# Layer 2 of a four-layer megakernel: who adds the exponentials, and in what order the small work beside them stands

## Chip, core and metric

The kernel runs on one core of one Trainium2 chip, as one launch. The metric is device time in microseconds, as the median of several executions. The tuned kernel before the change takes 3455.24 us (three runs, 3453.64 to 3456.24).

## What is computed

Input and output are `x` of shape (4, 256, 48, 48) in float32: four samples, 256 channels, 2304 positions. Four layers follow one another, each of the form x = x + layer(groupnorm(x)), with 32 groups and no affine part:

```python
# layer 0: attention with 8 heads of 64, q and k normalized, scale 10
sim = einsum('bhdi,bhdj->bhij', q, k) * 10; out = einsum('bhij,bhdj->bhid', softmax(sim), v)
# layer 1: 3x3 max pool, blur with stride 3 to 16x16, four depthwise 11x3 filters,
#          sigmoid gate, gate enlarged to 48x48 and multiplied onto the input
# layer 2: attention with one head of 64 (theta, phi, g), then W and batch norm over all samples
f = einsum('bnc,bcm->bnm', theta_x, phi_x) * 64 ** -0.5; y = einsum('bnm,bmc->bnc', softmax(f), g_x)
# layer 3: channel gate from means, depthwise 3x3, instance norm, leaky relu
```

The softmax is computed without subtracting a maximum: exponentials are multiplied with the values, and the result is divided by the sum of the exponentials.

## The kernel before

The attention of layers 0 and 2 is one long loop, `attend` (line 487). A unit is one block of 384 queries: in layer 0 for a pair of heads (96 units), in layer 2 for two query halves of one sample (12 units, three for each sample). A unit has nine groups of two key blocks of 128 keys. The pass for a group `t` issues, in this order: the scores of group `t` (`scores`, line 318: eight matmuls a key block pair on TensorE, one exponential of 128x768 for each block on ScalarE into one of eight `pt` buffers), then `add_up` of the group before (line 349: the sum of exponentials over the keys, kept elementwise in `acc`), then the jobs that are due, then the fills, and last `weigh` of the group before (line 337: exponentials times values). All engines run in this written order; nothing is reordered later. The fills are everything else: projections of the next pair or sample, layer 1 of other samples, group norms, statistics. A job in `due` or `fills` carries a rank; without one it is 5, and jobs of a pass are sorted by it. Only fills of a rank below 1 stand ahead of `add_up`; `lanes` are generators that are advanced by a step or more in each pass.

`add_up` has two forms. For a group in `paired`, GpSimd adds the group's two exponential tiles into `half` (line 355) and VectorE adds `half` to `acc` (line 370). For the others VectorE adds both tiles itself. In layer 0, sample 0 pairs the odd groups and samples 1 to 3 pair none. In layer 2, samples 0 to 2 pair all nine groups and sample 3 the odd ones (`l2_unit`, line 1293). The first addition of a unit is line 364.

At the end of a unit, `last` (line 462) copies the weighed values from PSUM (`take`), and places the rest: `total` (line 374) sums `acc` over partitions with matmuls and `invert`, `fold` and `divide` follow on VectorE and GpSimd with DMAs between. The last sample's units are "soon": `total_here` (line 425) sums `acc` with a matrix of ones and takes a reciprocal on VectorE. The very last unit is also "final"; its `total_here` folds and copies the row of sums on ScalarE ahead of the reciprocal.

Layer 1 of samples 0 to 2 runs beside layer 0. That of sample 3 runs beside layer 2 of samples 0 to 2, in four lanes (`l1_last`, line 1371): maxima and blur on VectorE (`maxima`, line 878), the filters as matmuls (`strips_pe`, line 999) on shifted copies that DMAs on SP's queue place in one of three buffers ("y", "t" and "w" in `ORDER3`, line 992), then `gated` (line 1123) and statistics for the next group norm. After that `follow` (line 1427) starts the layer 2 projection of sample 3 (`project2`, line 1151: `both` makes theta and phi from one product, `g` the values). The projection of sample 0 runs beside the last pair of layer 0, one slice of 384 positions in every ninth pass; there the slices come by DMA from a DRAM copy (`fetch`).

`w_stats` (line 1262) multiplies finished `y` with W into both `pj` PSUM tiles (there are only two) and takes VectorE's batch statistics of them. After the loop, the last unit's product, the merge of statistics and layer 3 follow.

Of the attention's inputs, `biased` (line 577) puts its one-column product into a column of the key projection's tile when `of_k` says that this tile belongs to the current pass, and into a tile of its own otherwise.

Of the kernel before, what the change touches and what calls it, by code (L numbers as in the profile page):

```python
# [78 lines left out]
def usual_path(  # L79
# [269 lines left out]
    def add_up(u, g):  # L349

        pts = [u["pt"][j] for j in range(g * G, (g + 1) * G)]
        terms = u.setdefault("terms", [])
        if g in u["paired"]:
            half = hpool.tile([P, 2, SL], F32, tag="half", name="half")
            nc.gpsimd.tensor_add(half, pts[0], pts[1])  # L355
            pts = [half]
            ready, u["terms"] = terms, pts
        else:
            ready, u["terms"] = terms + pts, []
        if g == NG - 1:  # L360
            ready, u["terms"] = ready + u["terms"], []
        if "acc" not in u and len(ready) > 1:
            u["acc"] = apool.tile([P, 2, SL], F32, tag="acc", name="acc")
            nc.vector.tensor_add(u["acc"], ready[0], ready[1])  # L364
            ready = ready[2:]
        if "acc" not in u:
            u["terms"] = ready + u["terms"]
            return
        for term in ready:
            nc.vector.tensor_add(u["acc"], u["acc"], term)  # L370
# [54 lines left out]
    def total_here(u):  # L425

        ps = pj_tile()
        for h, c in enumerate(HALVES):
            nc.tensor.matmul(ps[c, :SL], lhsT=ones, rhs=u["acc"][:, h, :], start=True, stop=True)
        u["rinv"] = rpool.tile([P, SL], F32, tag="rinv", name="rinv")  # L430
        if u.get("final"):
            fold(u, nc.vector)
            row = xsp.tile([P, NK, SL + 1], F32, tag="xs", name="lrow")[:, 0, :SL]
            nc.scalar.copy(row, ps[:, :SL])
        nc.vector.reciprocal(u["rinv"], ps[:, :SL])
        u["l"] = row if u.get("final") else ps

    def note(u):

# [22 lines left out]
    def last(u, t):  # L462

        take(u)
        if u.get("soon"):
            todo = [
                (fills, 1, lambda: total_here(u)), (due, 2, lambda: divide(u, nc.vector)),
            ]
            if u.get("final"):
                noted.append(lambda: note(u))  # L470
            else:
                todo.insert(1, (due, 2, lambda: fold(u, nc.vector)))
                todo.append((due, 2, lambda: note(u)))
            after = 3
        else:
            at_total = AT_TOTAL if "shift" in u["of"] else AT_CHUNK
            todo = [
                (fills, at_total, (4.1, lambda: total(u))), (due, AT_FOLD, lambda: fold(u, nc.gpsimd)),
                (due, AT_INVERT, lambda: invert(u)),
                (due, AT_DIVIDE, lambda: divide(u, nc.gpsimd)),  # L480
            ]
            after = AT_AFTER
        todo += [(fills, after, fn) for fn in u["after"]]
        for when, dt, fn in todo:
            when.setdefault(t + dt, []).append(fn)

    def attend(phases):


        groups = []  # L490
        for units, work, others in phases:
            for slot, fns in work.items():
                fills.setdefault(len(groups) + slot, []).extend(fns)
            st = {"others": [[gen, n, a, z, 0, 0] for gen, n, a, z in others], "at": 0}
            groups += [(u, g, st) for u in units for g in range(NG)]
        prev = None

        def lanes(some, st, t, ends):
            for lane in some:
                gen, n, a, z, done, ready = lane  # L500
                until = -(-n * (st["at"] + 1 - a) // (z - a))
                clock["final"] = final = st["at"] == z - 1
                while final or (done < until and t >= ready and not ends):
                    wait = next(gen, None)
                    if wait is None:
                        break
                    done, ready = done + 1, t + wait
                lane[4:] = done, ready

        def do(table, t, which=lambda rank: True):  # L510

            jobs = [job if isinstance(job, tuple) else (5, job) for job in table.pop(t, ())]
            table[t] = [job for job in jobs if not which(job[0])]
            for rank, fn in sorted((job for job in jobs if which(job[0])), key=lambda job: job[0]):
                fn()

                if rank in EVICTED:
                    take_taps(1)

        for t, (u, g, st) in enumerate(groups):  # L520
            for j in range(g * G, (g + 1) * G):
                scores(u, j)

            do(fills, t, lambda rank: rank < 1)
            if prev is not None:
                add_up(*prev)
            do(due, t)

            ends = prev is not None and prev[1] == NG - 1
            clock["t"], clock["slot"] = t, st["at"] % NG  # L530

            clock["early"] = True
            if clock["slot"] == AT_AFTER % NG:
                lanes([lane for lane in st["others"] if lane[1] == FREE], st, t, ends)
            do(fills, t)
            clock["early"] = False
            lanes(st["others"], st, t + 0.5, ends)
            st["at"] += 1
            if prev is not None:
                pu, pg = prev  # L540
                for j in range(pg * G, (pg + 1) * G):
                    weigh(pu, j)
                if pg == NG - 1:
                    last(pu, t)
            take_taps(QUOTA[clock["slot"]])
            prev = (u, g)
        pu, pg = prev
        add_up(pu, pg)
        for j in range(pg * G, (pg + 1) * G):
            weigh(pu, j)  # L550
        last(pu, len(groups))
        for t in sorted(set(due) | set(fills)):
            do(fills, t)
            do(due, t)
# [385 lines left out]
    def strips(b, k, norm, res):  # L940
# [50 lines left out]
    ROUNDS3 = (((0, 6), (6, 9)), ((9, 15),), ((15, 18),), ((18, 21),))  # L991
    ORDER3 = [
        (0, 1, "y"), (0, 2, "y"), (0, 3, "y"), (0, 0, "t"), (1, 1, "w"), (1, 0, "t"), (1, 2, "w"),
        (1, 3, "t"),
    ]
    FILLS_AT_ONCE = 8
    SETTLED = 3
# [122 lines left out]
        add()  # L1120
        yield 1

    def gated(b, k, norm, res):

        acc = res["acc"]
        gate = lp.tile([P, AS, AS], F32, tag="gate", name="gate")
        nc.vector.tensor_scalar(
            acc, acc, vec[:, V_M1, k : k + 1], inv1[:, k : k + 1], ALU.subtract, ALU.mult
        )
        yield 1  # L1130
        nc.scalar.activation(gate, acc, AF.Exp, bias=nb1[:, k : k + 1], scale=-1.0)
        yield 1
        nc.vector.tensor_scalar(gate, gate, 1.0, None, ALU.add)
# [9 lines left out]
        for i in range(4):  # L1143
            if i < 3:
                nc.vector.tensor_mul(xg[:, :, i], xg[:, :, i], up)
            if i > 0:
                nc.vector.tensor_add(xg[:, :, i - 1], xg[:, :, i - 1], up2)
            yield 1


    def project2(b, norm, s2):
# [43 lines left out]
        def both(s):  # L1195
# [15 lines left out]
                bias=at["bias"][theta, 0:1],  # L1211
            )
            nc.sync.dma_start(s2["k"][theta, cols], s2["k"][phi, cols])

        def g(s):
            ps = pj_tile()
            nj = SL // P
            for i in range(nj):
                for k in range(NK):
                    for c in HALVES:  # L1220
                        nc.tensor.matmul(
                            ps[c, i * D : (i + 1) * D],
                            lhsT=at["x"](s, k)[:, i * P + c.start : i * P + c.stop],
                            rhs=at["w"][:, k, 2, :], start=k == 0, stop=k == NK - 1,
                        )
            nc.scalar.copy(
                s2["v"][:, s * nj : (s + 1) * nj, :].rearrange("p j d -> p (j d)"),
                ps[:, : nj * D],
            )
            if b == 0 and s + 2 < NSL:  # L1230
                fetch(s + 2)

        return start, [
            [(1, lambda s=s: both(s)), (2 if b else 2.7, lambda s=s: g(s))] for s in range(NSL)
        ]

    Y = {}
# [55 lines left out]
    def l2_unit(b, c, s2):  # L1293
        return {
            "pt": {}, "qc": slice(c * SL, (c + 1) * SL), "of": s2, "after": [],
            "paired": PAIRED if b == B - 1 else range(NG), "scale": D ** -0.5,
            "soon": b == B - 1, "final": b == B - 1 and c == L2C - 1,
            "o": lambda: y_of(b)[:, c * SL : (c + 1) * SL],
        }
# [71 lines left out]
    def l1_last(b, ahead):  # L1371
# [29 lines left out]
        def gates():  # L1401
            for k in range(NK):
                yield from until(res[k], "summed")
                yield from gated(b, k, norm, res[k])
                yield from stats(k)
            yield from gn(b, norm2, [], [])

# [19 lines left out]
    def follow(start, slices, norm):  # L1427

        while "nb" not in norm:
            yield 1  # L1430
        yield 2
        start()
        yield 1
        for c in range(L2C):
# [71 lines left out]
    for b in range(B):  # L1506
        work, others = {}, []

        def stats(b, c):
            return [lambda k=k: w_stats(b, k, c) for k in range(NK)]  # L1510

        if b > 0:
            spread(work, stats(b - 1, 1), [4, 5])
# [38 lines left out]
        fn()  # L1552
    for s in range(NCH):
        projs[0]["values"](s)
    projs[1]["norms"]()
    attend(phases)
    last_y = [w_mul(B - 1, k, L2C - 1, wide=True) for k in range(NK)]
# [1477 lines left out]
```

## Time and profile before

| what | value |
|---|---|
| median of three runs | 3455.24 us |
| profiled execution, its own time | 3453.34 us |
| its span, first to last instruction | 3451.5 us |
| TensorE clock granted, mean | 0.997 |
| TensorE busy | 3384.6 us, 98% |
| VectorE busy | 2539.3 us, 74% |
| ScalarE busy | 2297.4 us, 67% |
| GpSimd busy | 828.0 us, 24% |
| exponentials, 128x768, line 330 | 1944 at 810 ns |
| additions of a tile, line 370 | 1368 at 1000 ns |
| additions of a half, line 370 | 171 at 1097 ns |
| pairs on GpSimd, line 355 | 189 at 1966 ns |

In the profile PE is TensorE, DVE VectorE, ACT ScalarE and POOL GpSimd. A group's row gives its line, engine and operation, its output and inputs, the shapes, the number of instructions, their busy time and mean in ns, and then the idle time of the engine ahead of them with what ended it. Busy time of VectorE or GpSimd includes time in which an instruction has begun and is held up. A row of the order of time gives start, duration, engine, line, operation, and in brackets the idle time ahead of it and who ended it. The span ends at 3451.5 us; layer 2's attention runs from 2870.57 to about 3285 us, and layer 3 after it.

### The profile page before, as it was taken

The numbers are of one execution on the slowest core, as the hardware profiler recorded it, in microseconds if no ns is written. First come the engines' busy times: TensorE is split into PE (matmuls) and PEld (weight loads), VectorE is DVE, ScalarE is ACT, GpSimd is POOL, SyncE is SP. The second block draws the span as 40 slices with busy tenths as digits, with TensorE's granted clock in tenths as the row PEclk, the third lists the DMA queues.
The fourth block names the chain that finished last, engine by engine and source line by source line (L and its number), as shares of the span: only waits on it lengthen the run. The fifth ranks groups of instructions, "written<-read, shape, count | busy, mean of one in ns | idle before, by whom it ended". The sixth has DMA issues, their size and how long they took to land. (4 is left out here: it accounts for less than half of the span.)

```text
span 3451.5 us, 89291 instructions
## 1 busy us (share of the span) xinstructions
PE 3384.6 (98%) x37966; PEld 1698.6 (49%) x37966; DVE 2539.3 (74%) x3298; ACT 2297.4 (67%) x3690; POOL 828.0 (24%) x734
## 2 busy tenths in 40 slices
PE   8999999999999999999999999999999999899988
PEld 5555555555545444544454445554444444444533
DVE  3455545568788788687888787878887878857777
ACT  5565655555886687557866885569768855454577
POOL 2433333320111111011110010101010114777434
PEclk9999999999999999999999999999999999999999
DMA  2211111111111111131111011111111110230067
GB/s 91 50 23 27 22 27 22 27 22 27 20 32 22 27 22 22 31 73 22 27 21 24 15 31 18 31 18 27 22 27 18 29 21 8 58 66 11 9 154 229
DMA packets 111593, 127.25 MB, mean 37 GB/s; under 512 B 42912, under 2 KB 101648, under 8 KB 110416
## 3 DMA queue, kind: packets, MB, share of 16 engines
q1 hardware_dynamic: 109936, 119.53, 17.3%
q8 instruction: 300, 4.92, 0.6%
q10 hardware_dynamic: 1248, 1.91, 0.2%
q14 instruction: 109, 0.89, 0.1%
HBM read 56.99 MB, written 11.80 MB: 20 GB/s over the span
## 5 line engine op out<-in xcount | busy, mean ns | idle before, releaser
L330 ACT ACTIVATE pt<-sc 128x768 f32<-128x768 f32 x1944 | 1473.6, 810 | 757.9 <-PE sc L324 751.4
L370 DVE TENSOR_TENSOR acc<-acc,pt 128x768 f32<-128x768 f32 x1368 | 1367.3, 1000 | 145.3 <-ACT pt L330 51.7
L344 PE MATMUL av<-pt,v 64*64 64x384 f32 x13824 | 1274.8, 484 | 0.0
L324 PE MATMUL sc<-q,k 64*64 64x384 f32 x13824 | 1270.0, 482 | 0.5 <-ACT pt L330 0.5
L324 PEld LDWEIGHTS sc<-q,k 64*64 64x64 f32 x13824 | 525.3, 133 | 589.6 <-issue 556.5
L344 PEld LDWEIGHTS av<-pt,v 64*64 64x64 f32 x13824 | 518.2, 133 | 568.4 <-issue 521.5
L421 POOL TENSOR_TENSOR o<-o,rinv 128x384 f32<-128x384 f32 x95 | 123.7, 1302 | 1710.1 <-DMA rinv<-rinv 1700.0
L355 POOL TENSOR_TENSOR half<-pt 128x768 f32<-128x768 f32 x189 | 370.7, 1966 | 488.0 <-ACT pt L330 405.3
L739 DVE SCALAR_TENSOR_TENSOR x<-pj,bo,x 128x384 f32<-128x384 f32 x192 | 118.5, 617 | 344.2 <-ACT row L388 186.9
L951 ACT ACTIVATE prod<-pd,wt 128x256 f32<-128x256 f32 x486 | 340.5, 761 | 0.2
L370 DVE TENSOR_TENSOR acc<-acc,half 128x768 f32<-128x768 f32 x171 | 187.5, 1097 | 167.8 <-POOL half L355 166.7
L625 PE MATMUL pj<-xs,w 128*128 128x384 f32 (+1 forms) x720 | 275.4, 505 | 0.0
L625 PEld LDWEIGHTS pj<-xs,w 128*128 128x128 f32 x720 | 124.1, 189 | 127.9 <-ACT v L664 34.3
L324 PE MATMUL sc<-qv,kd 64*64 64x384 f32 x1728 | 167.3, 492 | 2.9 <-ACT pt L330 2.8
L974 DVE TENSOR_REDUCE prod<-prod 128x256 f32<-128x1280 f32 x114 | 168.7, 1480 | 0.9 <-ACT prod L951 0.9
L344 PE MATMUL av<-pt,qv 64*64 64x384 f32 x1728 | 167.1, 490 | 0.0
L723 PE MATMUL pj<-o,wo 128*128 128x384 f32 (+1 forms) x384 | 161.4, 502 | 2.3 <-DVE x L739 2.0
L659 PEld LDWEIGHTS pj<-w,xs 128*128 128x128 f32 x1080 | 134.4, 191 | 24.2 <-issue 1.2
L364 DVE TENSOR_TENSOR acc<-pt 128x768 f32<-128x768 f32 x99 | 116.4, 1176 | 39.5 <-ACT pt L330 39.4
L659 PE MATMUL pj<-w,xs 128*128 128x128 f32 x1080 | 134.9, 275 | 0.0
L417 POOL TENSOR_TENSOR o<-raw 128x384 f32<-128x384 f32 x95 | 121.6, 1280 | 43.6 <-ACT raw L413 42.5
L413 ACT COPY raw<-av 128x768 f32<-128x768 f32 x108 | 86.4, 800 | 48.2 <-PE av L344 47.7
(304 smaller groups left out, 2227.6 us busy)
## 6 DMA issues: line engine op xcount, KB each, us to landing
xs<-in_x_dram SPq DMA_DIRECT2D x90, 384.0 KB
sh<-pad SPq DMA_DIRECT2D x126, 162.2 KB
rinv<-rinv SPq DMA_DIRECT2D x208, 94.5 KB
out_dram<-x SPq DMA_DIRECT2D x23, 384.0 KB
w<-in_wqkv_dram SPq DMA_DIRECT2D x32, 192.0 KB
x<-in_x_dram SPq DMA_DIRECT2D x4, 1152.0 KB
x<-in_x_dram SPq DMA_DIRECT2D x9, 384.0 KB
rinv<-ls SPq DMA_DIRECT2D x208, 1.5 KB
```

The source lines that it names most:

```text
L324: nc.tensor.matmul(ps[c * D : (c + 1) * D, h, :SL], lhsT=u["of"]["k"][r, j0 : j0 + D], rhs=u["of"]["q"][r, u["qc"]], start=True, stop=True,)
L330: nc.scalar.activation(pt, ps[:, :, :SL], AF.Exp, scale=u["scale"])
L344: nc.tensor.matmul(u["av"][h * D : (h + 1) * D, half, :SL], lhsT=value(u, j, h)[r], rhs=pt[r, h, :], start=j == 0, stop=j == JB - 1,)
L355: nc.gpsimd.tensor_add(half, pts[0], pts[1])
L370: nc.vector.tensor_add(u["acc"], u["acc"], term)
L417: eng.tensor_add(u["sum"], u["raw"][:, 0, :], u["raw"][:, 1, :])
L421: eng.tensor_mul(o, o, u["rinv"])
L625: nc.tensor.matmul(ps[:, :n], lhsT=at["w"][:, k, t, :], rhs=xs[s][:, k, :n], start=k == 0, stop=k == NK - 1,)
L659: nc.tensor.matmul(ps[:, i * P : (i + 1) * P], lhsT=xs[s][:, k, i * P : (i + 1) * P], rhs=at["w"][:, k, 2, :], start=k == 0, stop=k == NK - 1,
L723: nc.tensor.matmul(ps[:, :n], lhsT=wo[:, p, k * P : (k + 1) * P], rhs=o["o"][:, :n], start=True, stop=True,)
L951: nc.scalar.activation(bufs[n % 3][:, :, min(n, 1) + i].rearrange("p (r c) -> p r c", c=AS), pd[:, PAD + dr : PAD + dr + AS, PAD + dc : PA ...
L974: nc.vector.tensor_reduce(to, bufs[n % 3][:, :, : min(n, 1) + len(taps)], AX.X, ALU.add)
```

## The change

There are seven edits.

1. `l2_unit`: no group of layer 2 is paired any more. Every exponential tile is added by VectorE.
2. The last unit: its last group's two tiles are not added at all. `add_up` leaves them in `loose`, and `total_here` sums `acc` and both tiles with the matrix of ones, in six matmuls in one accumulation, issued after the weighing of group 7 and ahead of that of group 8. The copy of the row of sums and the fold come after the take.
3. `ORDER3`: the last shifted stack of sample 3's second half is placed in the "y" buffer instead of the "t" buffers.
4. `gated(brief=True)` for sample 3: four steps are merged into others, so the same instructions are issued over fewer passes; `follow` waits one pass instead of two.
5. `project2` for sample 0: in each slice `g` comes first (rank 1) and `both` second (rank 2.7); the fetch of the slice after next is issued by `both`.
6. `w_stats` of layer 2 gets rank 0.5, so its products and statistics stand ahead of `add_up`.
7. `of_k` is cleared before the second pair's `norms` ahead of the loop.

```diff
@@ add_up
         if g == NG - 1:
             ready, u["terms"] = ready + u["terms"], []
+            if u.get("final"):
+                u["loose"] = ready
+                return
@@ total_here
-        for h, c in enumerate(HALVES):
-            nc.tensor.matmul(ps[c, :SL], lhsT=ones, rhs=u["acc"][:, h, :], start=True, stop=True)
+        terms = [u["acc"], *u.get("loose", ())]
+        for i, term in enumerate(terms):
+            for h, c in enumerate(HALVES):
+                nc.tensor.matmul(
+                    ps[c, :SL], lhsT=ones, rhs=term[:, h, :], start=i == 0,
+                    stop=i == len(terms) - 1,
+                )
         u["rinv"] = rpool.tile([P, SL], F32, tag="rinv", name="rinv")
-        if u.get("final"):
-            fold(u, nc.vector)
-            row = xsp.tile([P, NK, SL + 1], F32, tag="xs", name="lrow")[:, 0, :SL]
-            nc.scalar.copy(row, ps[:, :SL])
         nc.vector.reciprocal(u["rinv"], ps[:, :SL])
-        u["l"] = row if u.get("final") else ps
+        u["l"] = ps
@@ last
         take(u)
+        if u.get("final"):
+            row = xsp.tile([P, NK, SL + 1], F32, tag="xs", name="lrow")[:, 0, :SL]
+            nc.scalar.copy(row, u["l"][:, :SL])
+            u["l"] = row
@@ attend, after the last pass
         add_up(pu, pg)
+        total_here(pu)
@@ ORDER3
-        (1, 3, "t"),
+        (1, 3, "y"),
@@ gated
-        yield 1
+        if not brief:
+            yield 1
...
-            yield 1
+            if not brief or i % 2:
+                yield 1
@@ project2
-            [(1, lambda s=s: both(s)), (2 if b else 2.7, lambda s=s: g(s))] for s in range(NSL)
+            [(1, lambda s=s: both(s)), (2, lambda s=s: g(s))] if b else
+            [(1, lambda s=s: g(s)), (2.7, lambda s=s: both(s))] for s in range(NSL)
@@ l2_unit
-            "paired": PAIRED if b == B - 1 else range(NG), "scale": D ** -0.5,
+            "paired": (), "scale": D ** -0.5,
@@ follow
-        yield 2
+        yield 1
@@ stats
-            return [lambda k=k: w_stats(b, k, c) for k in range(NK)]
+            return [(0.5, lambda k=k: w_stats(b, k, c)) for k in range(NK)]
@@ before the loop
+    of_k.clear()
     projs[1]["norms"]()
```

More of the change, by code (lines that the diff above doesn't have):

```diff
@@ L464, in last @@
         take(u)
+        if u.get("final"):
+            row = xsp.tile([P, NK, SL + 1], F32, tag="xs", name="lrow")[:, 0, :SL]
+            nc.scalar.copy(row, u["l"][:, :SL])
+            u["l"] = row
         if u.get("soon"):
             todo = [
-                (fills, 1, lambda: total_here(u)), (due, 2, lambda: divide(u, nc.vector)),
+                (due, 2, lambda: fold(u, nc.vector)), (due, 2, lambda: divide(u, nc.vector)),
             ]
@@ L471, in last @@
             else:
-                todo.insert(1, (due, 2, lambda: fold(u, nc.vector)))
+                todo.insert(0, (fills, 1, lambda: total_here(u)))
                 todo.append((due, 2, lambda: note(u)))
@@ L1121, in strips_pe, with gated @@
         yield 1
-    def gated(b, k, norm, res):
+    def gated(b, k, norm, res, brief=False):
         acc = res["acc"]
@@ L1213, in both @@
             nc.sync.dma_start(s2["k"][theta, cols], s2["k"][phi, cols])
+            if b == 0 and s + 2 < NSL:
+                fetch(s + 2)
         def g(s):
@@ L1229, in g @@
             )
-            if b == 0 and s + 2 < NSL:
-                fetch(s + 2)
         return start, [
-            [(1, lambda s=s: both(s)), (2 if b else 2.7, lambda s=s: g(s))] for s in range(NSL)
+            [(1, lambda s=s: both(s)), (2, lambda s=s: g(s))] if b else
+            [(1, lambda s=s: g(s)), (2.7, lambda s=s: both(s))] for s in range(NSL)
         ]
@@ L1403, in gates @@
                 yield from until(res[k], "summed")
-                yield from gated(b, k, norm, res[k])
+                yield from gated(b, k, norm, res[k], brief=True)
                 yield from stats(k)
```

## The prediction, on record before the run

> **What bounds the kernel now.** I read the page first, then the stretches of layer 2, then the groups and the order of time inside them. TensorE sets the span:
>
> ```profile
> PE 3384.6 (98%) x37966; PEld 1698.6 (49%) x37966; DVE 2539.3 (74%) x3298; ACT 2297.4 (67%) x3690; POOL 828.0 (24%) x734
> ```
>
> An edit that removes no matmul can therefore give back only TensorE's waits, 67 us at most in the whole span, and slow clock. Where they are, the stretches show (columns: stretch, length, then busy time of PE, PEld, DVE, ACT, POOL, then the granted clock and the DMA share):
>
> ```profile
> 2873.00:3005.00 132.00, 119.43 (x1427) 59.92 (x1421) 120.82 (x134) 64.93 (x98) 95.24 (x48) 0.99 0.16 31
> 3005.00:3202.00 197.00, 184.82 (x2282) 95.96 (x2278) 119.27 (x142) 98.32 (x153) 132.21 (x73) 0.97 0.22 42
> 3202.00:3284.00 82.00, 79.88 (x969) 44.24 (x964) 65.45 (x79) 43.10 (x58) 42.87 (x40) 1.00 0.04 5
> 3284.00:3300.00 16.00, 10.50 (x96) 6.28 (x90) 12.85 (x32) 8.57 (x6) 1.67 (x4) 1.00 0.00 0
> 2460.00:2592.00 132.00, 131.71 (x1440) 65.94 (x1432) 113.29 (x151) 78.86 (x127) 15.14 (x14) 1.00 0.13 20
> ```
>
> The first two are layer 2 of samples 0 to 2, with the last sample's layer 1 beside it; TensorE idles 12.6 and 12.2 us there. The last row is layer 0 with the same kind of layer 1 work, where no pair is added on POOL: 0.3 us of idleness. The difference stands in the groups (first row of each engine: layer 2's first stretch; last row: layer 0, 2400 to 2800 us):
>
> ```profile
> L370 DVE TENSOR_TENSOR acc<-acc,half 128x768 f32<-128x768 f32 x24 | 29.3, 1220 | 3.3 <-POOL half L355 3.0
> L355 POOL TENSOR_TENSOR half<-pt 128x768 f32<-128x768 f32 x33 | 73.5, 2239 | 21.2 <-ACT pt L330 13.0 <-DVE acc L370 8.0
> L370 DVE TENSOR_TENSOR acc<-acc,pt 128x768 f32<-128x768 f32 x217 | 215.6, 994 | 19.0 <-ACT pt L330 4.5 <-DVE acc L370 0.9
> ```
>
> One shape costs 1220 ns beside POOL's pairs and 994 without. In order of time it is plainer:
>
> ```profile
> 3134.54 2.56 DVE L1147 TENSOR_TENSOR x<-x,l1acc 128x768 f32<-128x768 f32 x1
> 3137.03 2.55 DVE L370 TENSOR_TENSOR acc<-acc,half 128x768 f32<-128x768 f32 x1
> 3139.50 1.02 DVE L1264 BATCH_NORM_STATS2 bst<-pj 128x6 f32<-128x384 f32 x2
> 3140.11 2.01 PE L1256 MATMUL pj<-y,Ww 64*64 64x384 f32 x8 [3.51 <-DVE bst L1264]
> ```
>
> Two operations of 0.95 us elsewhere take 2.55 us each, the statistics queue behind them, and TensorE waits 3.51 us for the two pj banks, then runs its next chunks slowly. Comparing TensorE's chunk starts with the usual distance of each kind (1.29 us for 16 attention matmuls), the lost time above 0.25 us sums to 34.7 us from 2873 to 3202: about 16 before 3005 and 18.7 after, slow clock included.
>
> **The Trainium skill.** "SBUF — State Buffer", section "Who interferes with whom", says that a VectorE instruction with two SBUF inputs and a GpSimd instruction that reads SBUF exclude each other, the second being held for the whole first. The 2.55 us against 0.95 agree. "GPSIMD Engine Reference", section 4.1, puts a two-input elementwise operation on GpSimd at about twice VectorE's time; the trace has about 1.8 us for an undisturbed pair against 0.95 to 1.0. "TensorE: Matmul & The Clock Gate", "What's actually happening", says that the clock falls after an idle window; the stretch with the longest waits has 0.97.
>
> **The change, part by part.**
>
> *Pairs.* For samples 0 to 2, nine POOL pairs and nine VectorE additions of a unit become 17 VectorE additions. One add costs 1.0 us (the 994 row). I cost a ledger per group of two key blocks: TensorE's time from the chunk distances, VectorE's from undisturbed rows. For the first 32 groups (2874 to about 3001, 127 us now): TensorE's chunks 112 us. VectorE: 61 adds x 1.0, and 49 us for the rest at undisturbed price (four half maxima of about 8.5 us, statistics, the first reciprocal of 2.5, small items): 110. What POOL still holds comes on top. In the 132 us stretch VectorE was busy 120.8; undisturbed its 28 adds would be 28 and the rest 49, so 44 us were waits, 0.46 us for each of POOL's 95 us. POOL keeps 95.2 - 73.5 = 21.7 us (fold, divide, shift, diagonals), some 9 us of VectorE. So VectorE needs 119 and becomes the limit here, with 2 us in which it waits itself: 121 against 127, **6 us** saved. Bounds: nothing left of the holds and lag absorbed by the eight pt buffers, 11; holds at 0.7 per us, 1.
>
> The second stretch is loaded only at the two gates. There the ledger's lag (adds 2.0 plus the gate's 2.5 us, then three 0.87 us operations a group, against 2.6 to 3.2 us of TensorE) climbs to about 6.4 and 7.5 us. Eight pt buffers let VectorE lag about three groups, 7.7 us, so I charge 2 us there. At the next statistics (lag 5) the two pj banks bind: about 3.5 us for them and the group norm's matmul just after. Unchanged projection waits take 1.3, the last projection 1.3, other small waits 2. That is 10 of 18.7: **8.7 us** saved, bounds 4 and 14.
>
> *Statistics ahead of additions* is what lets me charge so little: two bn_stats (0.94 us) no longer stand behind two adds (2.0). Queued behind them are now the adds; they wait for a product of the same group, with at least two groups of pt buffers to spare. In the last sample the statistics' waits (1.05 and 1.07 us in the trace) and smaller ones shrink, while four added adds per unit lie in VectorE's 16 us of idle time: **1.5 us**, bounds 0 and 3.
>
> *Shorter chain.* The last stack goes to the y buffer, which is free, so its product comes four groups earlier; its 16 DMAs, 11 us of issue on SP's queue, move ahead of two copies of sample 2's keys (kd). Those land about 11 us later, near 3098, and are first read some 8 us after that; without this cover TensorE would wait for them. The gates stand in fewer groups. The group norm's matmul comes eight groups earlier, and the six projections (2.8 us a pair) are spread over three groups instead of standing in one block at 3183. No work goes away; its gain is in the figures above (some 1 us of alternating waits), and its price is the gate lag, charged at 2.
>
> *g first beside layer 0.* TensorE's waits between 2700 and 2870 us:
>
> ```profile
> PE pj L1221 <- ACT qv L1209: 3.7, 6, 0.6
> ```
>
> Six waits of 0.62: ScalarE's two exponentials end about 1.5 us after the scores, two evictions of 0.58 follow, TensorE arrives after 2.08. With g first, TensorE does g (0.85) and an output product (0.74), 1.59 us; g's one eviction of 0.32 ends at about 1.85. The wait becomes 0.26: 6 x 0.36 = **2.2 us**, bounds 0 and 3.7. The fetch moves behind the projection, half a microsecond later in its group; the next slice is used two slots of some 28 us later, so it costs nothing.
>
> *The last total*, in order of time:
>
> ```profile
> 3282.98 0.95 DVE L370 TENSOR_TENSOR acc<-acc,half 128x768 f32<-128x768 f32 x1
> 3284.04 2.02 DVE L370 TENSOR_TENSOR acc<-acc,pt 128x768 f32<-128x768 f32 x2
> 3286.12 0.87 PE L429 MATMUL pj<-acc,ones 128*64 128x384 f32 x4 [1.59 <-DVE acc L370]
> 3287.54 2.56 DVE L435 RECIPROCAL rinv<-pj 128x384 f32<-128x384 f32 x1 [1.01 <-ACT lrow L434]
> ```
>
> Three adds (3 us) leave the chain; TensorE sums two more terms instead (2 x 0.7) ahead of the last weighing. Last exponential 3282.87, totals to 3285.0, reciprocal to 3287.7, weighing and take beside it, then fold, multiply, shift to 3289.2; the 13 warming matmuls (3.2 us) end at 3289.5. The next product starts there instead of at 3291.2: **1.7 us**, bounds 0.5 and 3.
>
> *Clearing of_k* takes another bank for one 1-column product before the attention: 0.
>
> Sum: 6 + 8.7 + 1.5 + 2.2 + 1.7 = 20.1 us. The profiled execution took 3453.34 us (span 3451.5); it becomes 3433.2. The median of the runs is 1.9 us above it: 3435.
>
> **The rivals.**
>
> 1. *All the cover holds.* Removing the holds takes every such wait: of 34.7 us only the projections' and the notes' (about 6) stay, 29 saved, with 1.5, 2.2 and an upper 3: 36, so 3419. For it: layer 0's row, 0.3 us idle with VectorE 113 of 132 busy. Against: the maxima are packed denser here, 119 in 121.
> 2. *The waits move into VectorE's queue.* In the first stretch nothing is saved, the gates' lag costs all but 2 of the second's, and the ends give half: about 4 us, 3451. For it: VectorE was busy 120.8 of 132 already. Against: a third of that was waiting.
> 3. *Slower: VectorE becomes the bound.* If an add stays at the 1.39 us that the paired first adds average in the first stretch, 60 x 0.39 = 23 us come on VectorE's path there, 17 us longer than now; the second loses 5, the ends give 5: 3472. It decides from about 1.33 us an add, where 60 x 0.33 - 6 equals the other gains of 14. Against: adds without an overlapping POOL operation took 1.0 in layer 0.
>
> **How the numbers follow.** Forecast 0.53 (its own range 3425 to 3446), rival 1 0.20, rival 2 0.18, rival 3 0.09. Half of rival 1 below and about as much above are left out: 3417 to 3450. Within 0.2% (6.9 us, about what a measurement of this kernel can tell from no change) lies most of rival 2; faster takes the forecast, rival 1 and the better third of rival 2: 0.80; same 0.13; slower 0.07.
>
> **What would show it.** Adds of layer 2 near 1.0 us; no pairs on POOL; VectorE still above 95% up to the second sample's statistics and TensorE idle about 7 us there; the wait before the last statistics of sample 2 near 3 us; g's waits replaced by about 0.26 us; the last reciprocal about 2.5 us after the last exponential. Wrong if the adds stay above 1.2, or if waits for pt exceed 5 us.

## The result and the profile after

The changed kernel takes 3426.32 us (median of four runs, 3424.51 to 3428.06), beside 3454.44 us for the kernel before on the same chip: ratio 0.9918, 95% interval [0.9901, 0.9936], or 28.1 us less. The forecast was 3435 us, with a range of 3417 to 3450. The profiled execution took 3426.86 us, with a span of 3425.0.

First the engine totals of the profile after:

```profile
PE 3379.8 (99%) x37974; PEld 1684.4 (49%) x37974; DVE 2542.0 (74%) x3389; ACT 2296.0 (67%) x3690; POOL 628.5 (18%) x641
```

TensorE has eight matmuls more and 26 us of span less; GpSimd has lost 93 instructions and 200 us; VectorE has 91 instructions more and is busy only 2.7 us longer. That last pair is the change in small: the added work cost VectorE hardly more than the holding up that it ended. The stretches of layer 2 in the changed kernel, which begins 8 us earlier (columns: stretch, length, busy time of PE, PEld, DVE, ACT, POOL, then clock, DMA share, GB/s):

```profile
2865.00:2992.00 127.00, 122.67 (x1462) 59.96 (x1458) 110.22 (x167) 65.44 (x100) 22.69 (x16) 0.97 0.16 33
2992.00:3178.00 186.00, 178.79 (x2251) 87.20 (x2244) 132.50 (x190) 98.13 (x152) 31.02 (x24) 1.00 0.23 44
3178.00:3257.00 79.00, 77.97 (x958) 35.99 (x952) 65.09 (x90) 43.08 (x58) 19.09 (x28) 1.00 0.04 5
```

TensorE now idles 4.3, 7.2 and 1.0 us there, where it idled 12.6, 12.2 and 2.1. Not all of the gain is idle time: of the 20.0 us that layer 2 gives in the table below, 17.0 are idle time of TensorE (29.6 us before, 12.6 after) and 3.0 are busy time of nearly the same matmuls (4732 and 4741 in the two records). The granted clock is 0.97 in the first stretch, with 4.3 us of idle time of which 3.1 are one wait, and 1.00 in the second, with 7.2 us in waits of at most 1.5; here it went with the longest single wait and not with their sum. VectorE is busy 110.2 of the first 127 us, 87%: it did not become the limit. Its additions over the three stretches together:

```profile
L373 DVE TENSOR_TENSOR acc<-acc,pt 128x768 f32<-128x768 f32 x190 | 187.9, 989 | 35.2 <-ACT pt L330 24.2
```

989 ns an addition, against 1220 ns for a half beside GpSimd's pairs in the first stretch before. TensorE's waits from 2690 to 3275 us (line, releaser: us in total, times, longest):

```profile
PE pj L247 <- DVE lsum L447: 3.1, 1, 3.1
PE pj L1234 <- ACT qv L1220: 2.2, 6, 0.4
PE sc L324 <- ACT pt L330: 1.9, 5, 0.7
...
PE pj L233 <- DVE bst L1276: 1.5, 1, 1.5
...
PE pj L1210 <- ACT qv L1220: 1.3, 3, 0.4
```

The waits for VectorE's batch statistics of layer 2's products (bst), 13.7 us before in three rows, are 1.5; two rows for `acc` that are left out have 1.1 and 1.0. To see where the time went I took four events from the order of time of each kernel: the first attention scores, the first scores of layer 2, the product after the last unit (line 1256 before, 1268 after), and the end of the span. Each cell is the length of a stage in us, in one profiled execution:

| kernel | start to scores | layers 0 and 1 | layer 2 | the rest | span |
|---|---|---|---|---|---|
| before | 44.0 | 2826.6 | 420.6 | 160.3 | 3451.5 |
| changed | 40.0 | 2822.8 | 400.6 | 161.7 | 3425.0 |
| difference | -4.0 | -3.8 | -20.0 | +1.4 | -26.5 |

The medians differ by 28.1, the profiled executions by 26.5; the experiments below show that the last stage alone varies by more than that gap.

### The profile page after: what moved, and what is told of

It reads as the page before. It is cut to its first block, busy times and chain, and to the rows that moved or that the text cites. A ratio compares the mean times of both kernels' runs of the same rounds, so it can differ in the third digit from the quotient of the medians.

```text
span 3425.0 us, 89305 instructions
## 1 busy us (share of the span) xinstructions
PE 3379.8 (99%) x37974; PEld 1684.4 (49%) x37974; DVE 2542.0 (74%) x3389; ACT 2296.0 (67%) x3690; POOL 628.5 (18%) x641
## 4 chain that ended last, share of the span: by engine, by line
PE 91%; DVE 5%; ACT 2%; issue 1%; SPq 0%; DMA 0%; POOL 0%; DVEq 0%; POOLq 0%; ACTq 0%
PE av L344 35%; PE sc L324 35%; PE pj L634 8%; PE pj L732 4%; PE pj L668 4%; DVE acc L373 2%; PE pj L386 1%; PE cv L1897 1%; PE pj L1210 1%; PE pj L1070 1%; PE pj L1268 0%; ACT sh L1766 0%; PE pj L1234 0%; SPq L1057 0%; ACT x L1909 0%
## 5 line engine op out<-in xcount | busy, mean ns | idle before, releaser
L373 DVE TENSOR_TENSOR acc<-acc,pt 128x768 f32<-128x768 f32 x1534 | 1526.3, 995 | 177.8 <-ACT pt L330 75.6
L355 POOL TENSOR_TENSOR half<-pt 128x768 f32<-128x768 f32 x96 | 176.0, 1833 | 377.2 <-ACT pt L330 331.5
L373 DVE TENSOR_TENSOR acc<-acc,half 128x768 f32<-128x768 f32 x96 | 91.7, 956 | 120.5 <-POOL half L355 120.3
L324 PE MATMUL sc<-qv,kd 64*64 64x384 f32 x1728 | 160.0, 485 | 1.9 <-ACT pt L330 1.9
L367 DVE TENSOR_TENSOR acc<-pt 128x768 f32<-128x768 f32 x108 | 126.5, 1171 | 34.3 <-ACT pt L330 34.1
```

What stands on the lines that cost most here:

```text
L324: nc.tensor.matmul(ps[c * D : (c + 1) * D, h, :SL], lhsT=u["of"]["k"][r, j0 : j0 + D], rhs=u["of"]["q"][r, u["qc"]], start=True, stop=True,)
```

## The experiments

The theory after the result: the two engines' additions excluded each other, and ending that gives most of the 20 us of layer 2; the other edits of layer 2 give little; and the early 7.8 us come from the banks of the projections (the two pj tiles in PSUM). Rivals: GpSimd's pairs cost by waits for its buffers and by writes rather than by reading; the statistics' order carries the gain; the 4 us at the start are not the clearing of `of_k`. Each ratio is taken against the kernel before on the same chip, whose medians lie between 3453.57 and 3454.74 us.

**Before, with the three edits at the ends** (b_ends: clearing, g first, last total).

```diff
+    of_k.clear()
-            [(1, lambda s=s: both(s)), (2 if b else 2.7, lambda s=s: g(s))] for s in range(NSL)
+            [(1, lambda s=s: both(s)), (2, lambda s=s: g(s))] if b else
+            [(1, lambda s=s: g(s)), (2.7, lambda s=s: both(s))] for s in range(NSL)
...
+            if u.get("final"):
+                u["loose"] = ready
+                return
```

> The kernel before with the three edits outside layer 2's additions: of_k cleared ahead of the loop, g first beside layer 0, and the shorter last total. Theory, read from the trace after: clearing gives 4.0 us (the value projection at 31 us without its five waits of 0.57, first scores at 40.0 instead of 44.0), g first 3.8, the last total about 1: 8 to 9 us together, 3446. Rival: those 4 us at the start come from the later edits in some other way; then the first scores stay at 44 and the kernel gains some 4 us.

Measured: 3444.45 us, ratio 0.9974 [0.9965, 0.9983]. The stages, in the order of the table: 39.9, 2822.4, 419.8, 159.1. So the start gives 4.1 us and layers 0 and 1 give 4.2. What is left in layer 2, 0.8 us, would be the last total's, but it is within chance: in b_clear below, layer 2 is 1.0 us longer than before without an edit there.

**Before, with unpaired groups alone** (b_pairs).

```diff
-            "paired": PAIRED if b == B - 1 else range(NG), "scale": D ** -0.5,
+            "paired": (), "scale": D ** -0.5,
```

> The kernel before with only the pairs of layer 2 taken off GpSimd. Theory (GpSimd's pairs hold up VectorE's two-input operations, and TensorE waits for VectorE): most of what layer 2 gained comes back with this edit alone, 12 to 17 us, so 3438 to 3443, and an addition costs about 1.0 us. Rival (the place of the statistics is what counts, pairs only move work): 0 to 4 us.

Measured: 3435.32 us, ratio 0.9944 [0.9927, 0.9961]: 18.8 us less, of the 28.1 of the whole change and above the 12 to 17 that I gave it. Layer 2 takes 402.1 us instead of 420.6: 18.5 us, without the new order of statistics and without the shorter chain.

**Changed, with the pairs restored** (a_pairs): the same lines the other way.

> The kernel after with the pairs of layer 2 put back on GpSimd. Theory of the pairs: 11 to 16 us of the 28 are lost, 3437 to 3442, and the longest waits of TensorE are for VectorE's statistics or additions again. Rival (the statistics' place): at most 4 us are lost.

Measured: 3443.73 us, ratio 0.9973 [0.9961, 0.9984]; layer 2 takes 419.3 us, 18.7 more than in the changed kernel. By the medians 17.4 us are lost, again above the 11 to 16 that I expected. The edit is worth the same in both surroundings, so there is hardly any interplay with the others, and 1.5 of the 20.0 us of layer 2 are left for the statistics, the chain and the last total together.

**Before, with the statistics ahead alone** (b_stats).

```diff
-            return [lambda k=k: w_stats(b, k, c) for k in range(NK)]
+            return [(0.5, lambda k=k: w_stats(b, k, c)) for k in range(NK)]
```

> The kernel before with only the batch statistics ahead of the additions. Theory of the pairs: an addition still costs 1.2 to 1.3 us and VectorE is late anyway; 1 to 5 us are saved. Rival (the statistics' place is what counts): 10 us or more, since the waits for bst were the longest.

Measured: 3456.53 us, ratio 1.0007 [0.9998, 1.0016]: nothing gained, a miss, and layer 2 takes 423.7 us, 3.1 more. TensorE's waits of this kernel, 2690 to 3300 us, show an exchange:

```profile
PE pj L429 <- DVE acc L370: 4.9, 3, 3.8
PE pj L233 <- DVE bst L1264: 4.1, 1, 4.1
PE pj L1163 <- DVE gn_nb L262: 3.8, 1, 3.8
```

With the rows of lines 1256 and 1061 (3.1 and 2.9), the waits for bst fall from 13.7 us to 10.1, but the totals now wait 4.9 us for `acc` (1.6 before) and the norm's product 3.8 (1.0). While VectorE was held, moving its work only changed who waited.

**Changed, with the statistics behind the additions again** (a_nostats): the same two lines the other way.

> The changed kernel with the statistics of layer 2's products back behind the additions of their group. Theory: once VectorE adds alone, two statistics stand behind two additions (2.0 us) in each group in which they fall, while VectorE already lags by two groups at the gates, so TensorE waits longer for a projection bank: 2 to 6 us slower than the changed kernel, 3428 to 3432 us. Rival: the banks come free early enough either way, as the same edit gave nothing in the kernel before; within 1 us of the changed kernel, 3425.5 to 3427.5 us.

Measured: 3425.43 us, ratio 0.9922 [0.9909, 0.9936]; layer 2 takes 401.1 us against 400.6. The rival held. Its waits, 2690 to 3300 us:

```profile
PE pj L1268 <- DVE bst L1276: 3.0, 2, 2.1
...
PE pj L233 <- DVE bst L1276: 1.7, 1, 1.7
```

With 0.4 at line 1070 that is 3.6 us more for bst, and in return the 1.9 us for exponentials and the 1.0 for the last total are gone and 0.4 of the wait at L386: 3.3 less. Again an exchange, and a miss for the theory.

**Changed, with the long chain of the last sample** (a_nochain).

```diff
-        (1, 3, "y"),
+        (1, 3, "t"),
...
-                yield from gated(b, k, norm, res[k], brief=True)
+                yield from gated(b, k, norm, res[k])
...
-        yield 1
+        yield 2
         start()
```

> The changed kernel with the long layer 1 chain of the last sample (last stack in a buffer of its own, gates over more groups, projections two groups after the norm). Theory: the chain's gain is that its projections do not stand in one block with alternating waits, about 1 us, and its price a lag at the gates of about 3 us that the changed kernel shows near 3110 us; so the kernel without it is between 2 us faster and 1 us slower than the changed one, 3424 to 3428 us. Rival: the late block of projections and the late norm cost what they cost in the kernel before, 3 to 6 us: 3429 to 3433 us.

Measured: 3426.12 us, ratio 0.9919 [0.9905, 0.9932], layer 2 in 400.8 us. Its waits for bst, for the norm and for the projections are 1.0, 1.6 and 0.8 us longer, those for exponentials and at L386 0.9 and 1.1 shorter. The first theory held: the shorter chain neither gives nor takes a measurable time.

**Changed, with GpSimd still adding each old pair into a buffer that nothing reads** (a_hold: extra work, nothing left out).

```diff
+        if u.get("idle") and (u["idle"] > 1 or g % 2):
+            half = hpool.tile([P, 2, SL], F32, tag="half", name="half")
+            nc.gpsimd.tensor_add(half, pts[0], pts[1])
```

> The kernel after, and GpSimd still adds each pair that it added before, into a buffer that nobody reads; VectorE adds all tiles itself. Theory (a GpSimd instruction that reads SBUF holds VectorE's two-input ones): an addition costs 1.2 us or more, VectorE needs some 140 us in the first stretch of 127, and the kernel is 20 to 45 us slower than the one after, no faster than the one before: 3446 to 3471. Rival (only the amount of work on each engine counts, or who waits for whom): nothing waits for these additions, so 3426 stays within 3 us.

Measured: 3509.6 us, ratio 1.0158 [1.0141, 1.0175]: 83 us more than the changed kernel, far beyond the 20 to 45 that I gave it; layer 2 takes 485.2 us, 84.6 more. The same 190 additions, from 2865 to 3345 us in this kernel:

```profile
L376 DVE TENSOR_TENSOR acc<-acc,pt 128x768 f32<-128x768 f32 x190 | 258.1, 1359 | 19.2 <-ACT pt L330 7.6
```

258.1 us instead of 187.9. The additions alone keep VectorE busy 70 us longer; in all it is busy 121 us longer in layer 2 (434.7 instead of 313.9). Of TensorE's 84.6 us, 52.8 are idle time and 31.8 are slower matmuls, with a granted clock of 0.92 instead of 0.99. In order of time, GpSimd first, then VectorE:

```profile
2902.79 2.32 POOL L355 TENSOR_TENSOR half<-pt 128x768 f32<-128x768 f32 x1 [5.49 <-ACT pt L330]
2905.37 2.23 POOL L355 TENSOR_TENSOR half<-pt 128x768 f32<-128x768 f32 x1 [0.26 <-ACT pt L330]
```

```profile
2899.81 2.02 DVE L376 TENSOR_TENSOR acc<-acc,pt 128x768 f32<-128x768 f32 x2
...
2903.35 5.07 DVE L376 TENSOR_TENSOR acc<-acc,pt 128x768 f32<-128x768 f32 x2
...
2912.44 2.01 DVE L376 TENSOR_TENSOR acc<-acc,pt 128x768 f32<-128x768 f32 x2
```

Two additions take 2.0 us where GpSimd is idle, and 5.07 where it adds. The two engines need not read the same tile. In the kernel before, `x<-x,l1acc` took 2.56 us at 3134.54 (shown in the prediction) while GpSimd added exponentials:

```profile
3133.89 4.87 POOL L355 TENSOR_TENSOR half<-pt 128x768 f32<-128x768 f32 x2 [0.96 <-DVE acc L364]
```

GpSimd is also a second reader of the exponentials' buffers here. That has a share of its own: ScalarE waits 9.0 us for GpSimd's `half` to release them, and 27.4 us for VectorE's `acc` (none and 3.7 in the changed kernel). How much of the 83 us comes from this can't be told in this kernel. Additions were lengthened without a shared tile in the kernel before, too: 1220 ns for `acc` and `half` in the first stretch.

**Changed, with two GpSimd memsets of that buffer in place of each pair** (a_write: extra work, nothing left out).

```diff
+            nc.gpsimd.memset(half, 0.0)
+            nc.gpsimd.memset(half, 1.0)
```

> The kernel after, and GpSimd writes the same unread buffer twice with a constant in place of each pair's addition: about as busy, but it reads nothing. Theory (reads exclude each other): an addition stays at 1.0 us and the time within 4 us of 3426. Rival (any work of GpSimd holds VectorE up): as slow as with the unread additions.

Measured: 3426.44 us, ratio 0.9918 [0.9902, 0.9935], the changed kernel's own time. GpSimd is busy 70.5 us of the first stretch instead of 22.7, and the additions, 2865 to 3257 us, do not notice. (Over layer 2 it is busy 207.0 us, against 282.5 in a_hold and 73.4 in the changed kernel.)

```profile
L377 DVE TENSOR_TENSOR acc<-acc,pt 128x768 f32<-128x768 f32 x190 | 188.9, 994 | 34.9 <-ACT pt L330 23.9
...
L355 POOL MEMSET half<- 128x768 f32 x93 | 69.0, 742 | 0.4
```

So it is not GpSimd's being busy, nor its writing of this buffer: it is its reading of SBUF. The Trainium skill says the same ("SBUF — State Buffer", section "Who interferes with whom"): a VectorE instruction with two SBUF inputs contends with a GpSimd instruction that reads SBUF, "not with one that only writes it". These two runs agree: 1359 ns beside reads, 994 beside writes and 989 in the changed kernel, where GpSimd does its small work alone.

**Before, with the clearing of `of_k` alone** (b_clear).

> The kernel before with of_k.clear() ahead of the attention, and nothing else. Theory: the old tile of the last key projection held one of the two projection banks, so that the value projections waited five times 0.57 us and ran slower between; without it the attention starts 4.0 us earlier and the kernel ends 4 us earlier, ratio 0.9988 (3450.4 us). Rival, the prediction's own step: the tile holds nothing that matters, ratio 1.000, and the 4.0 us that the attention of the changed kernel starts earlier come from somewhere else.

Measured: 3450.76 us, ratio 0.9991 [0.9982, 0.9999], so 3 us, between 0.3 and 6; the first scores start at 39.87 instead of 43.96 us, and every other stage is as before within about 1 us. The order of time on TensorE, of the kernel before and of the changed one:

```profile
31.33 1.50 PE L659 MATMUL pj<-w,x 128*128 128x128 f32 x12
33.40 1.60 PE L659 MATMUL pj<-w,x 128*128 128x128 f32 x12 [0.57 <-ACT v L664]
```

```profile
31.50 8.20 PE L668 MATMUL pj<-w,x 128*128 128x128 f32 x72
```

Before, each value projection waits for the copy of the one before it, as it must with a single bank; after, all six run in one piece. The tile of the last key projection, which `biased` was still to write into after the values, kept the second bank.

**Changed, with the last sample's note, fold and divide ahead of the additions** (a_note; the note takes the sum and the minimum of a unit's normalizer from its pj tile).

```diff
-            else:
-                todo.insert(0, (fills, 1, lambda: total_here(u)))
-                todo.append((due, 2, lambda: note(u)))
+            else:
+                todo = [
+                    (fills, 1, lambda: total_here(u)), (fills, 2, (0.2, lambda: note(u))),
+                    (fills, 2, (0.3, lambda: fold(u, nc.vector))),
+                    (fills, 2, (0.4, lambda: divide(u, nc.vector))),
+                ]
```

> The kernel after, and in the last sample's units the sums of the normalizer, the fold and the division stand ahead of the pass's additions, the sums first. In the profile after TensorE waits 3.1 us in the first unit of layer 2 for the pj bank that these sums read, behind two additions of 1.96 us, and then runs slowly. Theory: the wait falls to 1 us or less and 2 to 4 us are gained, 3422 to 3424. Rival: VectorE is late there anyway because of its reciprocal of 2.56 us: less than 1 us.

Measured: 3425.72 us, ratio 0.9915 [0.9899, 0.9932]: 0.6 us by the medians and none in layer 2 (400.7 us), a miss. It aimed at the longest wait left, at the first unit of layer 2. The order of time of the changed kernel, VectorE and then TensorE:

```profile
2867.72 2.56 DVE L439 RECIPROCAL rinv<-pj 128x384 f32<-128x384 f32 x1 [1.14 <-PE pj L434]
2870.19 1.96 DVE L373 TENSOR_TENSOR acc<-acc,pt 128x768 f32<-128x768 f32 x2
...
2874.06 0.15 DVE L447 TENSOR_TENSOR lsum<-lsum,two 128x1 f32<-128x1 f32 x1
```

```profile
2870.28 0.91 PE L732 MATMUL pj<-o,wo 128*128 128x384 f32 x2
2874.29 0.56 PE L247 MATMUL pj<-gn_sq,gmat 128*128 128x2 f32 x2 [3.09 <-DVE lsum L447]
```

and TensorE with the note ahead:

```profile
2871.05 0.35 PE L247 MATMUL pj<-gn_sq,gmat 128*128 128x2 f32 x2
2874.67 0.94 PE L735 MATMUL pj<-o,wo 128*128 128x384 f32 x2 [3.27 <-DVE x L751]
```

The product that had waited 3.09 us runs at once, and the very next one waits 3.27: its bank is freed by `x<-pj`, and that now stands behind the additions. The wait was handed to the next product. So the rival's size was right, but not its reason, the reciprocal.

**Changed, with g first for samples 1 to 3 too** (a_gall).

```diff
-            [(1, lambda s=s: both(s)), (2, lambda s=s: g(s))] if b else
-            [(1, lambda s=s: g(s)), (2.7, lambda s=s: both(s))] for s in range(NSL)
+            [(1, lambda s=s: g(s)), (2 if b else 2.7, lambda s=s: both(s))] for s in range(NSL)
...
-            for _, fn in slices[c] + slices[c + L2C]:
+            for _, fn in sorted(slices[c] + slices[c + L2C], key=lambda job: job[0]):
```

> The kernel after with g ahead of theta and phi for samples 1 to 3 too. In the profile after, six waits of 0.37 and three of 0.42 are left there. Theory, as beside layer 0: g's single eviction of 0.32 is done before the bank is needed, 3 to 4 us are gained, 3422 to 3423. Rival: with two slices in one pass both banks are then in evictions of theta and phi and a wait comes later: 0 to 1 us.

Measured: 3419.39 us, ratio 0.9898 [0.9882, 0.9915]. The waits at L1234 and L1210, 3.5 us in the changed kernel, are gone, those for exponentials grow from 1.9 to 3.0, and layer 2 takes 395.9 us, 4.7 less: half of that is idle time of TensorE and half is busy time. The other 2.3 us of the difference lie in the last stage, where nothing was edited, so 4.7 is what the edit is shown to give. That is still more than the 3 to 4 of the theory.

**Both of these together** (best).

> The changed kernel with g first for samples 1 to 3 too and with the last sample's note, fold and divide ahead of the additions. Theory: g first gives its 6.9 us and the note 0.6 us, since they concern different waits: 3418.8 us, ratio 0.9896. Rival: with the note earlier the wait only moves to the next eviction, so that nothing is added to g first: 3419.4 us or up to 1 us more.

Measured: 3419.39 us, ratio 0.9902 [0.9886, 0.9917]; layer 2 in 396.0 us. The rival held: the note adds nothing. The version with g first everywhere beats both kernels: 34 to 35 us less than before, and 6.9 less than the changed one by the medians, of which 4.7 are in layer 2.

## Why the prediction was right, and where its steps were not

The forecast was faster by 20.1 us and the profiled executions differ by 26.5. Equal events in the two traces give each term: how much earlier the changed kernel is at the first scores (4.0 us), at the first scores of layer 2 (7.8), at the ends of units in the middle of layer 2 (15.2 at the fifth, 23.9 at the ninth), at the end of the last exponential and at the product that follows the last total (27.5 and 27.85).

| step of the prediction | forecast, us | measured, us |
|---|---|---|
| clearing `of_k` | 0 | 4.0 |
| g first beside layer 0 | 2.2 | 3.8 |
| pairs and chain, first stretch | 6 | 7.4 |
| pairs and chain, second stretch | 8.7 | 8.7 |
| last sample | 1.5 | 3.6 |
| the last total | 1.7 | 0.3 |
| the rest | 0 | -1.3 |
| sum | 20.1 | 26.5 |

The border between the two stretches is drawn at the end of the fifth unit. At my own border, 3001 us in the kernel before, the changed kernel is 13.1 us ahead, and one group later, after a wait for statistics, 15.8. So the two rows trade some 2 us with each other, and that each is close to its forecast is in part chance; their sum, 14.7 forecast and 16.1 measured, is the better test.

*Pairs: right.* The mechanism held with its price, as the two one-edit runs (18.5 and 18.7 us of layer 2) and the pair a_hold and a_write show. An addition costs 1.01 us in the first stretch and 0.99 in the second, where I took 1.0.

*First stretch: the limit was named wrongly.* The undisturbed ledger, 110 us of VectorE, was right to the microsecond: 110.22. The step that failed is the 9 us of residual holds that I added for GpSimd's other work: they did not come, so VectorE was 87% busy instead of above 95%. I had taken 0.46 us of hold for each busy microsecond of GpSimd from pairs alone; fold, divide, shift and diagonals, 22.7 us in the changed kernel, cost nothing visible at that rate. My bound without any holds was 11 us, and the trace shows about 12 gained by the end of the fifth unit, of which 4.45 were lost again in the first unit: TensorE waits 3.09 us for `lsum`, and 16 matmuls of the next groups take 2.84 and 1.98 us, where they take 1.52 and 1.47 before. I had put no wait there; it and the overcharge for the holds nearly cancel, so the 6 us came close by luck. Two additions, 1.96 us together, stand between the reciprocal and the note, where none stood before; in the kernel with unpaired groups alone the same wait is 3.1 us, where it was 1.2.

*Second stretch: right in the gates' lag, and in sum partly by chance.* At layer 1's gates, where VectorE falls behind with its additions, I charged 2 us; the trace has four waits for exponentials and one for `acc` between 3110 and 3117 us (lines 324 and 386), about 2.3 us; the first and the last of them:

```profile
3110.06 0.88 PE L324 MATMUL sc<-qv,kd 64*64 64x384 f32 x8 [0.40 <-ACT pt L330]
...
3116.72 0.54 PE L386 MATMUL pj<-acc,step 128*32 128x96 f32 x16 [1.07 <-DVE acc L373]
```

The 3.5 us at the last statistics were too much: 1.5 at line 233 is what is left. What makes up for these 2 us in the sum was not looked for.

*Statistics and chain: the reason was wrong.* "Statistics ahead of additions is what lets me charge so little" fell: without it the changed kernel is as fast. So is it without the shorter chain. The statistics exchange waits of nearly the same size, 3.6 us against 3.3; the chain's waits, 3.4 against 2.0, change the time just as little.

*g first: mis-sized by one reading.* I let the exponentials end about 1.5 us after the scores. In the trace they end 1.0 us after them (scores to about 2701.5, exponentials to 2702.50), the copy of g ends at 2702.79, and TensorE comes for the bank at 2703.10. Nothing is left of the six waits of 0.62 us, where I kept 0.26 each: 3.7 instead of 2.2.

*Clearing: the failed step.* "Takes another bank for one 1-column product: 0" priced the product and not the tile. With the old tile in `of_k`, one of the two `pj` banks stays taken until `biased` has run, through all six value projections. The five waits of 0.57 us stood in the trace of before.

*The last total: mis-sized.* The order of time on TensorE and VectorE in the changed kernel:

```profile
3256.71 0.87 PE L434 MATMUL pj<-acc,ones 128*64 128x384 f32 x4 [1.01 <-DVE acc L373]
...
3257.41 1.46 PE L434 MATMUL pj<-pt,ones 128*64 128x384 f32 x8
...
3258.92 2.56 DVE L439 RECIPROCAL rinv<-pj 128x384 f32<-128x384 f32 x1 [1.66 <-PE pj L434]
...
3260.25 3.17 PE L200 MATMUL sc<-gmat 128*128 128x128 f32 x26
...
3263.35 0.88 PE L1268 MATMUL sc<-y,Ww 64*64 64x384 f32 x8
```

The last exponential ends at 3255.35. I had the totals finished 2.1 us later; they are finished at 3258.87, 3.5 later, because `acc` of the group before is ready only at 3256.7. The weighing and the 13 warming matmuls (26 in the trace) queue behind, and their end sets the product, 0.3 us earlier after the last exponential than before. Shorter warming was not tried.

*The last sample* gave 3.6 us where I took 1.5, with 3 as the upper bound. No run tells its pairs from its statistics.

Of the rivals, the slower one was real as a mechanism: I gave an addition that stays at 1.39 us a time of 3472. With additions at 1.36 us, a_hold takes 3510. Its layer 2 is 36 us longer than before up to the end of the fifth unit, where I had 17, and 21 us longer from there to the ninth, where I had 5. That ledger had no other operation of VectorE held and no slower matmuls; but a_hold also has the second reader, so its numbers test the rival's kind and not its size. The prediction's rejection of it stands, for the overlap needs GpSimd to read.

## What to carry to other kernels

Work that is given to GpSimd is not free for VectorE if it reads SBUF while VectorE runs operations with two inputs there: compare one shape's mean with and without the other engine beside it, and cost the removed help at the undisturbed price. Before pricing an allocation at the instruction that uses it, ask how long the handle keeps a bank from others; here the sign was five waits of one size, each for the copy of the tile just before. And in three runs (b_stats, a_nostats, a_note) moving work within VectorE's queue only exchanged one wait for others of about the same size. Moving TensorE's own jobs was different: g first gave time in both places where it was tried.

## What was not expected

A pair that nobody reads costs 0.9 us (83 us for 93 pairs of 2.13 us each), nearly a whole VectorE addition, and over a third of that is TensorE's slower matmuls between longer waits. And the last stage, the same code in every kernel, took between 159.0 and 164.2 us in the profiled executions, so a difference of 2 us between two kernels is read from the edited stage and not from the span.
